# Selective-scan steps of 16 channels by 8 states in place of 8 channels by 16 states

## The chip, the cores and the metric

The kernel runs on one core of a Trainium2 chip. The metric is the device time of one execution in microseconds (us). The kernel before takes 7516.72 us (median of three runs, 7508.94 to 7519.74). All data is float32.

## The reference, cut to what matters

Four layers follow each other on an image of 2 x 64 channels x 96 x 96 pixels. Layer 0 is a non-local attention block, layer 3 a dynamic 3x3 filter; the change leaves both alone. Layer 1 holds one Mamba block over the 9216 pixels of each image. Layer 2 holds four: a forward and a backward one along the columns, then a forward and a backward one along the rows (sequences of 96). Each Mamba block computes, per channel of 128 and per state of 16:

```python
xc = silu(conv1d(xm) + convd_b)                    # 128 channels
dt, Bm, Cm = split(x_proj(xc), [4, 16, 16])
dt = softplus(dt @ dt_proj_w.T + dt_proj_b)        # 128 channels
A = -exp(A_log)                                    # 128 x 16
def step(h, inp):                                  # h: channels x states
    dA_t, dBx_t, C_t, x_t = inp
    h = exp(dt_t[:, None] * A) * h + dt_t[:, None] * B_t[None, :] * x_t[:, None]
    return h, einsum("ds,s->d", h, C_t)
y = (scan of step) + xc * Dp
out = (y * silu(z)) @ out_proj_w.T
```

## The kernel before

The sequence axis is the free axis. A *unit* is 768 positions (`CH`) of one Mamba block; there are 24 units in layer 1 and 96 in layer 2, 48 of them over columns and 48 over rows. In layer 2 units come in pairs, forward and backward, that share one image and one normalised input, so `image_0`, `image_1`, `norm_mean`, `norm_root`, `norm_scale` and the tail run once per pair; in layer 1 they (or `norm_centre`, `norm_square`, `norm_affine`) run for every unit. Below, an even unit is the first of a pair.

The recurrence of 128 channels x 16 states is 2048 rows, but an engine has 128 partitions. A unit is therefore worked off in 16 *steps* (`STEPS`), eight for each half of its positions (`HALF`, 384). A step of the kernel before has 8 channels by 16 states in each of its two 384-element parts. For each step:

- SyncE issues two DMAs (`read`, L912) that bring dt and dt times x of the step's channels from a DRAM copy (`rows`) to the tile `spread` (6 buffers);
- ScalarE makes the decay exp(dt A) with two exponentials (`decay`, L919) into the tile `h` (9 buffers), three steps ahead (`DECAY`);
- VectorE multiplies by B (`inputs`, L929): it reads `spread` and the PSUM bank `B`, and writes one of two PSUM tiles `place`, even steps one, odd steps the other; both products of a pair of steps stand before its two scans;
- VectorE runs the recurrence (`scan`, L944; L940 in layer 1), h = h * decay + place, in place in `h`;
- GpSimd multiplies h by C (L945);
- TensorE adds the states up into the PSUM bank `y` (`gather`, L954) with a 128x128 product for each part, two steps late, and first, once a half, the product with D (L951).

The bank `B` is filled by TensorE twice a unit (`shared`, L923), after the last product that reads its old content.

Everything else that a unit needs is cut into pieces with an offset in steps (`PIECES`, L995): a piece at offset o of a unit is issued at that unit's first step plus o, so that several units are in work at once. `run` (L1035) writes this order out by hand, step by step, and each engine takes its own instructions in this order. Pieces whose name is in `reads` come before the others of the same step. Offset -27, say, stands at step 5 of the unit two before. The pieces on the path of the softplus are `step_mm`, `step_read`, `step_exp` (three ScalarE operations), `step_log`, then on GpSimd `step_kept`, `step_sum`, `step_dt` (its sums) and `step_u` (dt times x), then `step_write` (L891, two DMAs to `rows`).

All matrix products outside `B`, `y` and `place` share one PSUM tile `m`: `open` hands it out, and the next product into it waits until ScalarE has read the last one. Eight PSUM banks are in use: four for `place`, one for `B`, one for `y`, two for `m`.

Of the kernel before, what the change touches and what calls it, by code (L numbers as in the profile page):

```python
# [35 lines left out]
NMAMBA = 5  # L36

# [34 lines left out]
def setup(ctx, tc, x, cols, mats, dtw):  # L72
# [42 lines left out]
    k.minus = const.tile([P, 1], FP, name="minus")  # L115
    nc.vector.memset(k.minus, -1.0)
# [91 lines left out]
def layer0_direct(k, scale, bias, pre):  # L208
# [9 lines left out]
    with (  # L218
# [19 lines left out]
        def product(lhsT, rhs, m, n):  # L238
            p = bank("m")[:m, :n]
            nc.tensor.matmul(p, lhsT=lhsT, rhs=rhs, start=True, stop=True)  # L240
            return p
# [321 lines left out]

class Carver:
# [16 lines left out]
def mamba_tables(k, pool):  # L581
# [4 lines left out]
    G = P // 8  # L586
    t = SimpleNamespace()

    t.member = pool.tile([P, 8], FP, name="member")
    nc.vector.reduce_sum(t.member, k.ident.rearrange("p (g i) -> p i g", i=8), axis=AX.X)  # L590
    t.group = pool.tile([P, 2, G], FP, name="group")
    for j in range(2):
        nc.vector.reduce_sum(t.group[:, j], k.ident.rearrange("p (g i) -> p g i", i=8), axis=AX.X)

    pair = pool.tile([P, 2, P], FP, name="pair")
    nc.vector.tensor_copy(pair, k.ident.unsqueeze(1).to_broadcast([P, 2, P]))
    pair = pair.rearrange("p j c -> p (j c)")
    t.gather = [pair[:, P - 8 * n : 2 * P - 8 * n] for n in range(G)]

# [8 lines left out]
def scratch(k, t, pool):  # L608


    G = P // 8
    t.turned = pool.tile([P, G, G], FP, name="turned")
    two = t.group.rearrange("p j g -> p (j g)")
    for n in range(G):
        k.nc.vector.tensor_copy(t.turned[:, n], two[:, G - n : 2 * G - n])
    t.placed = pool.tile([P, D_STATE, 8], FP, name="placed")
    t.rates = pool.tile([P, P // 8, P // 8], FP, name="turned_rates")


def mamba_weights(k, w, pool, product, tables, i):  # L620
# [4 lines left out]
    G = P // 8  # L625


# [3 lines left out]
    nc.vector.tensor_mul(  # L631
        tables.placed,
        tables.member.unsqueeze(1).to_broadcast([P, D_STATE, 8]),
        a.unsqueeze(2).to_broadcast([P, D_STATE, 8]),
    )
    p = product(tables.placed.rearrange("p s i -> p (s i)"), tables.group[:, 0], P, G)
    yield
    nc.vector.tensor_mul(tables.rates, tables.turned, p.unsqueeze(1).to_broadcast([P, G, G]))
    w.rates = pool.tile([P, G], FP, name=f"rates{i}")
    nc.vector.reduce_sum(w.rates, tables.rates, axis=AX.X)  # L640
# [23 lines left out]
    bc = pool.tile([P, 2, D_STATE, 8], FP, name=f"bc{i}")  # L664
    for j in range(2):
        at = DT_RANK + j * D_STATE
        nc.vector.tensor_copy(bc[:, j], x_w[:, at : at + D_STATE].unsqueeze(2).to_broadcast([P, D_STATE, 8]))
    w.gate_w = in_w[:, P:]
    w.bc = [bc[:, j].rearrange("p s i -> p (s i)") for j in range(2)]
# [5 lines left out]
class Mamba:  # L675
# [15 lines left out]
    STEPS = P // 8  # L691
    READ = 5
    DECAY = 3

# [14 lines left out]
    def product(self, lhsT, rhs, m, n):  # L709
        p = self.ps_m.tile([P, 2 * NB], FP, tag="m", name="mm")[:m, :n]  # L710
        self.nc.tensor.matmul(p, lhsT=lhsT, rhs=rhs, start=True, stop=True)
        return p
# [137 lines left out]
    def step_read(self, u):  # L850
# [5 lines left out]
        u.kept = self.by_half(self.work("kept", bufs=1))  # L856
# [4 lines left out]
    def step_exp(self, u):  # L861
        nc = self.nc
        nc.scalar.activation(u.e, u.e, AF.Exp, scale=-1.0)
        nc.scalar.activation(u.kept, u.e, AF.Identity, bias=1.0)
        nc.scalar.activation(u.kept, u.kept, AF.Identity, bias=self.k.minus)  # L865
# [5 lines left out]
    def step_kept(self, u):  # L871
        self.nc.gpsimd.tensor_sub(u.kept, u.e, u.kept)  # L872

    def step_sum(self, u):
        self.nc.gpsimd.tensor_add(u.log, u.log, u.kept)
# [159 lines left out]
    def run(self, units, first, n_first, other):  # L1035


        for u in units:
            u.dtu, u.h = {}, {}
# [340 lines left out]
```

## Time and profile before

| | us |
|---|---|
| median of three runs | 7516.72 |
| profiled execution, time | 7506.74 |
| profiled execution, span | 7504.8 |
| attention (layer 0), about the first 2440 of the span | 2440 |
| Mamba units (layers 1 and 2), up to about 7420 | 4980 |
| VectorE busy in the stretch 3500 to 7300 (3800 us) | 3786.7 |
| GpSimd busy in the same stretch | 3582.1 |
| TensorE busy in the same stretch | 3333.8 |
| ScalarE busy in the same stretch | 3042.1 |

The span runs from the first to the last instruction; the time has a few us around it. Busy times of one engine don't overlap with themselves, but those of different engines do. A mean duration of one instruction is longer than the distance at which the engine takes the next one, because the engines start an instruction before the last has drained: where work stands back to back, the distance from start to start is what counts, and a timeline shows it.

### The profile page before, as it was taken

How to read it: one execution, taken by the hardware profiler on the slowest of the kernel's cores; microseconds unless marked ns; L12 is line 12 of the kernel's file. 1: busy time of each engine (PE TensorE's matmuls, PEld its weight loads, DVE VectorE, ACT ScalarE, POOL GpSimd, SP SyncE). 2: the span in 40 equal slices, each digit the busy share in tenths (PEclk: the TensorE clock that was granted, in tenths of full speed). 3: DMA queues.
4: the chain of work that ended last, by engine and by line, in shares of the span. 5: the costliest groups of instructions: out<-in, count | busy, mean ns of one | idle time of the engine just before them, and what ended most of it. 6: DMA issues, size and time to landing. Idle time of an engine off the chain costs nothing.

```text
span 7504.8 us, 104657 instructions
## 1 busy us (share of the span) xinstructions
PE 6801.0 (91%) x34802; PEld 3032.7 (40%) x34802; DVE 6906.7 (92%) x5972; ACT 5303.9 (71%) x7420; POOL 4855.2 (65%) x3218
## 2 busy tenths in 40 slices
PE   9999999999998888888888888888988888888887
PEld 3333333333333344444444444444444444444443
DVE  6777877888886899999999999999999999999999
ACT  5555555555555778777877788888888787787783
POOL 0000000000001799998999999999999999999995
PEclk9999999999998999999999999999999999999999
DMA  1000000000000889998999999999999999999995
GB/s 46 1 1 1 1 1 1 3 5 6 5 6 30 292 320 336 320 326 302 352 331 344 343 354 355 347 355 350 352 355 352 349 353 350 353 353 346 351 356 198
DMA packets 593910, 1727.49 MB, mean 230 GB/s; under 512 B 65992, under 2 KB 67148, under 8 KB 592848
## 3 DMA queue, kind: packets, MB, share of 16 engines
q1 hardware_dynamic: 591912, 1717.69, 62.9%
q8 instruction: 275, 4.51, 0.2%
q10 hardware_dynamic: 1448, 3.04, 0.1%
q14 instruction: 275, 2.25, 0.1%
HBM read 1522.68 MB, written 197.79 MB: 229 GB/s over the span
## 4 chain that ended last, share of the span: by engine, by line
PE 10%; DMA 10%; issue 10%; POOL 9%; ACT 7%; DVE 6%; SPq 1%; DVEq 0%; ACTq 0%; POOLq 0%
DMA spread<-rows 8%; POOL h L945 6%; PE y L954 6%; ACT h L919 3%; DMA rows<-dtu 2%; DVE place L929 2%; DVE h L944 2%; PE mm L725 2%; PE conv L827 1%; POOL dtu L878 1%; PE y L951 1%; DVE xa L1279 1%; POOL dtu L882 1%; SPq L912 0%; PE B L923 0%
## 5 line engine op out<-in xcount | busy, mean ns | idle before, releaser
L945 POOL TENSOR_TENSOR h<-h,C 128x768 f32<-128x768 f32 x1920 | 3455.5, 1821 | 231.3 <-DVE h L944 197.0
L954 PE MATMUL y<-h,pair 128*128 128x384 f32 x7680 | 2818.1, 508 | 170.0 <-POOL h L945 168.5
L944 DVE TENSOR_TENSOR_SCAN h<-h,place 128x768 f32<-128x768 f32 x1536 | 2608.2, 1742 | 0.0
L919 ACT ACTIVATE h<-spread,xa 128x384 f32<-128x384 f32 x3072 | 1755.0, 608 | 481.0 <-DMA spread<-rows 441.3
L954 PEld LDWEIGHTS y<-h,pair 128*128 128x128 f32 x7680 | 1480.1, 198 | 1400.7 <-POOL h L945 418.2
L312 ACT ACTIVATE e<-f_exp 128x1024 f32<-128x1024 f32 x1296 | 1257.7, 1022 | 987.6 <-PE f_exp L298 987.6
L929 DVE TENSOR_TENSOR place<-spread,B 128x768 f32<-128x768 f32 x1920 | 1736.5, 953 | 96.2 <-PE B L923 48.6
L323 PE MATMUL y<-e,xb 64*64 64x512 f32 x10368 | 1232.1, 590 | 0.0
L298 PE MATMUL f_exp<-theta,phi 64*64 64x512 f32 x10368 | 1230.0, 589 | 2.0 <-DVE xb L283 1.5
L401 DVE TENSOR_TENSOR acc_e<-acc_e,e 128x1024 f32<-128x1024 f32 x612 | 771.6, 1261 | 300.7 <-ACT e L312 283.3
L337 POOL TENSOR_TENSOR ys<-ys,y_one 128x512 f32<-128x512 f32 x36 | 46.0, 1277 | 1456.2 <-DVE ys L336 1456.2
L410 DVE TENSOR_TENSOR acc_e<-acc_e,e 128x1024 f32<-128x1024 f32 x612 | 810.7, 1325 | 65.2 <-DVE acc_e L401 1.8
L940 DVE TENSOR_TENSOR_SCAN h<-h,state,place 128x384 f32<-128x384 f32 x768 | 714.6, 993 | 3.2 <-ACT h L919 3.1
L323 PEld LDWEIGHTS y<-e,xb 64*64 64x64 f32 x10368 | 393.6, 133 | 728.2 <-issue 722.4
L298 PEld LDWEIGHTS f_exp<-theta,phi 64*64 64x64 f32 x10368 | 395.5, 133 | 715.0 <-issue 703.0
L362 POOL TENSOR_TENSOR xa<-xa,t_att 64x512 f32<-64x512 f32 x36 | 54.3, 1508 | 755.9 <-ACT t_att L360 735.2
L919 ACT ACTIVATE h<-spread,rates 128x384 f32<-128x384 f32 x768 | 433.9, 608 | 113.1 <-DMA spread<-rows 99.8
L951 PE MATMUL y<-raw,xa 128*128 128x384 f32 x384 | 207.2, 626 | 213.3 <-ACT yg L961 185.7
L827 PE MATMUL conv<-xn,xa 64*128 64x384 f32 (+3 forms) x1536 | 275.3, 497 | 11.8 <-DVE xa L1161 4.1
L725 PE MATMUL mm<-raw,xa 128*128 128x384 f32 x768 | 279.4, 486 | 0.1
L872 POOL TENSOR_TENSOR kept<-dtu,kept 128x768 f32<-128x768 f32 x120 | 218.6, 1822 | 64.9 <-ACT kept L865 64.2
L832 ACT ACTIVATE raw<-conv,cols 128x768 f32<-128x768 f32 x120 | 108.2, 901 | 187.2 <-PE conv L827 143.5
(219 smaller groups left out, 5622.5 us busy)
## 6 DMA issues: line engine op xcount, KB each, us to landing
spread<-rows SPq DMA_DIRECT2D x3840, 384.0 KB, 5.6
rows<-dtu SPq DMA_DIRECT2D x240, 768.0 KB, 5.1
image<-pre SPq DMA_DIRECT2D x11, 384.0 KB, 2.3
xb<-image SPq DMA_DIRECT2D x11, 384.0 KB, 7.1
xa<-in_x SPq DMA_DIRECT2D x1, 2304.0 KB, 22.5
out<-xa ACTq DMA_DIRECT2D x7, 240.0 KB, 2.0
out<-xa SPq DMA_DIRECT2D x1, 1200.0 KB, 4.3
xa<-in_x SPq DMA_DIRECT2D x3, 384.0 KB, 11.6
```

What stands on the lines that cost most here:

```text
L298: nc.tensor.matmul(f[rows_of(half), bass.ts(side, NB)], lhsT=phi[at, m * P + half * C : m * P + (half + 1) * C], rhs=theta[at, bass.ts(i, ...
L312: nc.scalar.activation(e, f, AF.Exp)
L323: nc.tensor.matmul(ys[half][rows_of(side)], lhsT=g[at, m, :], rhs=e[at, bass.ts(side, NB)], start=m < 2, stop=m >= KEYS - 2,)
L401: nc.vector.tensor_add(block.acc, block.acc, es[0])
L410: nc.vector.tensor_add(block.acc, block.acc, es[1])
L725: self.nc.tensor.matmul(o, lhsT=lhsT, rhs=x, start=n == 0, stop=n == len(terms) - 1)
L919: self.nc.scalar.activation(h[:, bass.ts(q, HALF)], dt, AF.Exp, scale=u.w.rates[:, n : n + 1])
L929: self.nc.vector.tensor_mul(bx, x, self.B.unsqueeze(1).to_broadcast([P, 2, HALF]))
L940: nc.vector.tensor_tensor_scan(h[:, at], h[:, at], bx[:, at], state[:, q : q + 1], ALU.mult, ALU.add)
L944: nc.vector.tensor_tensor_scan(h[:, way], h[:, way], bx[:, way], 0.0, ALU.mult, ALU.add)
L945: nc.gpsimd.tensor_mul(h2, h2, u.C[:, bass.ts(half, HALF)].unsqueeze(1).to_broadcast([P, 2, HALF]))
L954: self.nc.tensor.matmul(self.y, lhsT=self.t.gather[n], rhs=rhs, start=False, stop=stop)
```

## The change

A step now has 16 channels (`SPAN`) by 8 states (`GROUP`) in each part. The two halves of the states are `PARTS`: steps 0 to 3 of a half take the first eight states of all channels, steps 4 to 7 the last eight.

- The tile `spread` of a half's step m serves step m and step m + 4, so a unit has 16 DMA reads instead of 32; each reads 16 rows and repeats each eight times. `rows` is written once.
- `B` and C have two patterns. TensorE fills `B` four times a unit, and C is made in two pieces (`c_mm_0`, `c_mm_1`), one for each half of the positions, with a ScalarE copy each.
- The states of a part are added up by products with 32 output rows, written to four 32-row quarters of `y`; the gathers of two steps are issued together, at odd steps.
- The softplus sums (e - kept etc.) are no longer three GpSimd operations: TensorE multiplies four terms with the identity (`sum_mm`, eight products) and ScalarE copies the sum back (`sum_read`). The kept term is made with its sign turned.
- For steps 7 and 15 (`ASIDE`) the product with B is made by GpSimd, three steps ahead. [...] The product goes to the SBUF tile `bx`, and the decay of these steps goes to `place`, one step ahead.
- The offsets of most pieces change.

Not shown: the tables and weights of the new layout (`mamba_tables`, `scratch`, `by_state`, `mamba_weights`), which are made once, and the state tile of layer 1, whose shape follows.

```diff
+SPAN, BLOCKS, PARTS = 16, 8, 2
+GROUP = P // SPAN
+TILE = 32
...
+def products(nc, p, lhsT, rhs, m, n):
+    each = lhsT if isinstance(lhsT, list) else [lhsT]
+    for j, one in enumerate(each):
+        nc.tensor.matmul(p[:m, j * n : (j + 1) * n], lhsT=one, rhs=rhs, start=True, stop=True)
+    return p[:m, : len(each) * n]
+def channels(block):
+    first = TILE * (block % 4) + SPAN * (block // 4)
+    return slice(first, first + SPAN)
...
+    held = pool.tile([P, 3 * SPAN], FP, name="held")
+    nc.vector.memset(held, 0.0)
+    own = k.ident.rearrange("p (i g) -> p i g", g=GROUP)
+    nc.vector.reduce_sum(held[:, SPAN : 2 * SPAN], own, axis=AX.X)
+    t.gather = [held[:, SPAN:], held[:, :TILE]]
...
-    STEPS = P // 8
-    READ = 5
+    STEPS = 16
+    READS = {2: 0, 3: 1, 5: 2, 6: 3}
     DECAY = 3
+    ASIDE = (7, 15)
...
+    def sum_mm(self, u):
+        u.p = self.mm([(self.k.ident, lambda j, t=t: t[:, j]) for t in (u.e, u.kept, u.log, u.dt)])
+    def sum_read(self, u):
+        self.nc.scalar.copy(u.dt, self.by_half(u.p))
...
-        u.rows = self.dram.tile([2 * P, 2 * CH], FP, tag="rows", name="rows")
-        for j in range(2):
-            self.nc.sync.dma_start(out=u.rows[j * P : (j + 1) * P], in_=u.both)
-    def c_mm(self, u):
-        u.p = self.mm([(u.w.bc[1], self.halves(u.xc))])
-    def c_read(self, u):
-        u.C = self.work("C")
-        self.nc.scalar.copy(u.C, u.p)
+        u.rows = self.dram.tile([P, 2 * CH], FP, tag="rows", name="rows")
+        self.nc.sync.dma_start(out=u.rows, in_=u.both)
...
+    def c_mm(self, u, half):
+        sides, u.p = self.open()
+        for part, p in enumerate(sides):
+            x = u.xc[:, bass.ts(half, HALF)]
+            self.nc.tensor.matmul(p, lhsT=u.w.bc[1][part], rhs=x, start=True, stop=True)
+    def c_read(self, u, half):
+        u.C[half] = self.by_half(self.work("C"))
+        self.nc.scalar.copy(u.C[half], self.by_half(u.p))
...
-    def read(self, u, step):
-        half, turns = self.turns(step)
-        u.dtu[step] = self.work("spread", 2 * CH, bufs=6)
-        for q, n in enumerate(turns):
-            row = u.rows[8 * n : 8 * n + P, bass.ts(half, CH)]
-            self.nc.sync.dma_start(out=u.dtu[step][:, bass.ts(q, CH)], in_=row)
+        part, m = divmod(m, BLOCKS // 2)
+        return half, part, m
+    def read(self, u, half, m):
+        d = u.dtu[half, m] = self.work("spread", 2 * CH, bufs=6)
+        for q in range(2):
+            rows = u.rows[channels(2 * m + q), bass.ts(half, CH)]
+            self.nc.sync.dma_start(
+                out=d[:, bass.ts(q, CH)], in_=rows.unsqueeze(1).to_broadcast([SPAN, GROUP, CH])
+            )
+    def spread(self, u, step, a):
+        half, _, m = self.turns(step)
+        return u.dtu[half, m].rearrange("p (q a t) -> p q a t", q=2, a=2)[:, :, a]
+    def place(self, step):
+        return self.places[step % 2][1].rearrange("p (q t) -> p q t", q=2)
+    def room(self, u, step):
+        u.h[step] = self.by_half(self.work("h", bufs=9))
+        u.decay[step], u.bx[step] = u.h[step], self.place(step)
+        if step in self.ASIDE:
+            u.decay[step], u.bx[step] = self.place(step), self.by_half(self.work("bx", bufs=1))
     def decay(self, u, step):
-        h = u.h[step] = self.work("h", bufs=9)
-        for q, n in enumerate(self.turns(step)[1]):
-            dt = u.dtu[step][:, q * CH : q * CH + HALF]
-            self.nc.scalar.activation(h[:, bass.ts(q, HALF)], dt, AF.Exp, scale=u.w.rates[:, n : n + 1])
-    def shared(self, u, half):
-        self.nc.tensor.matmul(self.B, lhsT=u.w.bc[0], rhs=u.xc[:, bass.ts(half, HALF)], start=True, stop=True)
-    def inputs(self, u, step):
-        bx = self.places[step % 2][1].rearrange("p (q t) -> p q t", q=2)
-        x = u.dtu[step].rearrange("p (q a t) -> p q a t", q=2, a=2)[:, :, 1]
-        self.nc.vector.tensor_mul(bx, x, self.B.unsqueeze(1).to_broadcast([P, 2, HALF]))
+        _, part, m = self.turns(step)
+        dt = self.spread(u, step, 0)
+        for q in range(2):
+            rate = u.w.rates[:, part, 2 * m + q : 2 * m + q + 1]
+            self.nc.scalar.activation(u.decay[step][:, q], dt[:, q], AF.Exp, scale=rate)
+    def shared(self, u, half, part):
+        x = u.xc[:, bass.ts(half, HALF)]
+        self.nc.tensor.matmul(self.B, lhsT=u.w.bc[0][part], rhs=x, start=True, stop=True)
+    def b_copy(self, u):
+        u.B = self.work("Bs", HALF, bufs=1)
+        self.nc.scalar.copy(u.B, self.B)
+    def inputs(self, u, step, engine, B):
+        B = B.unsqueeze(1).to_broadcast([P, 2, HALF])
+        engine.tensor_mul(u.bx[step], self.spread(u, step, 1), B)
...
     def gather(self, u, step):
-        half, turns = self.turns(step)
-        if turns[0] == 0:
+        half, part, m = self.turns(step)
+        if part == m == 0:
             self.nc.tensor.matmul(self.y, lhsT=u.w.direct, rhs=u.xc[:, bass.ts(half, HALF)], start=True, stop=False)
-        for q, n in enumerate(turns):
-            rhs, stop = u.h[step][:, bass.ts(q, HALF)], n == self.STEPS - 1
-            self.nc.tensor.matmul(self.y, lhsT=self.t.gather[n], rhs=rhs, start=False, stop=stop)
...
+            block = 2 * m + q
+            y = self.y[bass.ts(block % 4, TILE)]
+            stop = part == PARTS - 1 and block >= BLOCKS // 2
+            self.nc.tensor.matmul(y, lhsT=self.t.gather[block // 4], rhs=u.h[step][:, q], start=False, stop=stop)
...
-        (-56, "image_0"),
+        (-54, "image_0"),
+        (-53, "norm_centre"),
         (-52, "image_1"),
-        (-51, "norm_centre"),
-        (-49, "norm_square"),
+        (-52, "norm_square"),
         (-47, "norm_mean"),
-        (-45, "norm_root"),
+        (-46, "norm_root"),
         (-38, "norm_scale"),
         (-36, "norm_affine"),
         (-27, "conv"),
         (-25, "conv_read"),
-        (-25, "gate_mm"),
-        (-23, "gate_read"),
-        (-22, "silu"),
-        (-21, "step_mm"),
+        (-23, "gate_mm"),
+        (-21, "gate_read"),
+        (-21, "silu"),
+        (-20, "step_mm"),
         (-19, "step_read"),
         (-18, "step_exp"),
-        (-17, "step_kept"),
         (-17, "step_log"),
-        (-17, "c_mm"),
-        (-15, "c_read"),
-        (-15, "step_sum"),
-        (-11, "step_dt"),
-        (-9, "step_u"),
-        (-6, "step_write"),
+        (-16, "sum_mm"),
+        (-15, "sum_read"),
+        (-14, "step_u"),
+        (-11, "step_write"),
+        (-1, "c_mm_0"),
+        (0, "c_read_0"),
+        (2, "c_mm_1"),
+        (3, "c_read_1"),
+        (3, "b_copy"),
         (10, "y_half"),
+        (11, "b_copy"),
         (18, "y_read"),
         (19, "y_gate"),
-        (25, "tail_0"),
-        (26, "tail_1"),
-        (27, "tail_read"),
+        (23, "tail_0"),
+        (23, "tail_1"),
+        (25, "tail_read"),
...
         for n in range(begin, len(steps) + end + 1):
             s = n % self.STEPS
-            if at(n + self.READ):
-                self.read(*at(n + self.READ))
+            if s % 8 in self.READS and at(n - s % 8 + 8):
+                u, step = at(n - s % 8 + 8)
+                self.read(u, step // 8, self.READS[s % 8])
+            if at(n + 1) and at(n + 1)[1] in self.ASIDE:
+                self.decay(*at(n + 1))
             if at(n + self.DECAY):
-                self.decay(*at(n + self.DECAY))
+                u, step = at(n + self.DECAY)
+                self.room(u, step)
+                if step in self.ASIDE:
+                    self.inputs(u, step, self.nc.gpsimd, u.B)
+                else:
+                    self.decay(u, step)
+            pieces(n, False)
             if at(n):
                 u = at(n)[0]
                 if s % 2 == 0:
-                    self.inputs(u, s)
-                    self.inputs(u, s + 1)
+                    for step in (s, s + 1):
+                        if step not in self.ASIDE:
+                            self.inputs(u, step, self.nc.vector, self.B)
                 self.scan(u, s)
-                if s == 6:
-                    self.shared(u, 1)
+                if s % 4 == 2 and s < 14:
+                    self.shared(u, *divmod(s // 4 + 1, PARTS))
             if s == 14 and at(n + 2):
-                self.shared(at(n + 2)[0], 0)
-            for late in self.lates(s):
-                if at(n - late):
-                    self.gather(*at(n - late))
-            for late in (False, True):
-                for is_late, offset, name in table[s]:
-                    i = (n - offset) // self.STEPS
-                    if is_late == late and (0 if n >= 0 else 1) <= i < len(units) and units[i]:
-                        getattr(self, name)(units[i])
-                if s in self.OTHER and n >= 0 and not late:
-                    next(other, None)
+                self.shared(at(n + 2)[0], 0, 0)
+            if s % 2 and at(n - 2):
+                self.gather(*at(n - 3))
+                self.gather(*at(n - 2))
+            if s in self.OTHER and n >= 0:
+                next(other, None)
+            pieces(n, True)
```

More of the change, by code (lines that the diff above doesn't have):

```diff
@@ L238, in product @@
         def product(lhsT, rhs, m, n):
-            p = bank("m")[:m, :n]
-            nc.tensor.matmul(p, lhsT=lhsT, rhs=rhs, start=True, stop=True)
-            return p
+            return products(nc, bank("m"), lhsT, rhs, m, n)
         def projections(theta, phi, g, sides):
```

127 lines of the change are left out of this document (63 added, 64 removed).

## The prediction

> **What bounds the kernel now.** First the busy times by stretch (length, then busy us and instructions of PE, PEld, DVE, ACT, POOL, then PEclk, DMA share, GB/s), for a stretch in layer 2:
>
> ```profile
> 4500.00:5500.00 1000.00, 884.77 (x2660) 440.16 (x2659) 997.83 (x796) 815.57 (x1215) 950.44 (x561) 0.96 0.96 352
> ```
>
> VectorE never rests (998 of 1000), GpSimd, DMA and TensorE come close, ScalarE has 18% to spare. Then VectorE's timeline (start, length, then what):
>
> ```profile
> 5003.68 1.81 DVE L929 TENSOR_TENSOR place<-spread,B 128x768 f32<-128x768 f32 x2
> 5005.38 3.39 DVE L944 TENSOR_TENSOR_SCAN h<-h,place 128x768 f32<-128x768 f32 x2
> 5008.69 1.81 DVE L929 TENSOR_TENSOR place<-spread,B 128x768 f32<-128x768 f32 x2
> ```
>
> From start to start: two products 1.70, two scans 3.31, so 0.85 and 1.655 each and 40.1 for a unit's 16 steps. In layer 1 two steps take 5.35 (four half scans 3.64), 42.8 a unit. Of ScalarE and TensorE I need the same distances, for their queues:
>
> ```profile
> 5003.12 0.84 ACT L863 ACTIVATE dtu<-dtu 128x768 f32<-128x768 f32 x1
> 5003.99 0.84 ACT L864 ACTIVATE kept<-dtu 128x768 f32<-128x768 f32 x1
> 5004.87 0.94 ACT L865 ACTIVATE kept<-kept,minus 128x768 f32<-128x768 f32 x1
> 5005.71 1.10 ACT L919 ACTIVATE h<-spread,xa 128x384 f32<-128x384 f32 x2
> 5006.73 0.83 ACT L869 ACTIVATE log<-dtu 128x768 f32<-128x768 f32 x1
> 5007.46 2.12 ACT L919 ACTIVATE h<-spread,xa 128x384 f32<-128x384 f32 x4
> 5009.48 0.78 ACT L898 COPY C<-mm 128x768 f32<-128x768 f32 x1
> 5010.16 1.12 ACT L919 ACTIVATE h<-spread,xa 128x384 f32<-128x384 f32 x2
> ...
> 5029.78 1.28 ACT L841 ACT_TABLE_LOAD   x1
> 5031.07 1.49 ACT L841 ACTIVATE raw<-raw 128x1536 f32<-128x1536 f32 x1
> 5032.58 1.28 ACT L842 ACT_TABLE_LOAD   x1
> 5033.87 1.12 ACT L919 ACTIVATE h<-spread,xa 128x384 f32<-128x384 f32 x2
> 5035.02 1.61 ACT L990 ACTIVATE xb<-mm,cols 64x768 f32<-64x768 f32 x1
> ```
>
> The exponentials of a step ("decay") take 1.02, e and kept 2.59 (5003.12 to 5005.71), the logarithm 0.73, a copy from PSUM 0.68, silu with its two table loads 4.09.
>
> ```profile
> 5003.85 1.45 PE L725 MATMUL mm<-raw,xa 128*128 128x384 f32 x4
> 5005.14 2.74 PE L954 MATMUL y<-h,pair 128*128 128x384 f32 x8
> ...
> 5029.18 1.50 PE L725 MATMUL mm<-yg,xa 128*64 128x384 f32 x4
> 5030.61 1.48 PE L725 MATMUL mm<-xb,xa 64*64 64x384 f32 x2
> ```
>
> A product is two instructions: two products 1.29, so 0.645 each; a half of the tail over columns 2 x 1.41. A handover between engines is 0.2: conv's 16 instructions, 5019.38 on, end at 5022.11 by their distance, and ScalarE starts at 5022.31.
>
> **What the change takes from VectorE.** Two products a unit: 2 x 0.85 = 1.70, and nothing is added, so 38.4 in layer 2. Over 120 units that is 204 us, if VectorE never waits. The rest of this part is whether it does.
>
> **GpSimd.** Three sums go, two products come: at 1.77 from start to start, 16 times C, two products, dt times x, the gate and half a norm are 20.5 x 1.77 = 36.3 of 38.4. It has room.
>
> **DMA.** Half the reads and writes; the share 0.96 falls to about a half. VectorE waited for `spread` only 47 us in all (the group's line), so at most that is won, at least nothing: ScalarE's DMA waits (441 us) lay beside a busy VectorE. I take 0. Against it stands that the reads for m = 2 and 3 wait for the products of steps 4 and 5 and that `step_write` stands between them in SP's queue; the slack of about three steps (7 us) before ScalarE needs them covers the 5.6 to landing, and the excess over it would be paid once a half without it.
>
> **The gathers.** Four products on four quarters of the array's columns. No row has 128x32. Two ends: all serial, 4 x 0.645 = 2.6; all at once, 0.65. Nearest row, 64x64 products on four quarters in layer 0:
>
> ```profile
> 1000.38 1.90 PE L298 MATMUL f_exp<-theta,phi 64*64 64x512 f32 x16
> 1002.10 1.90 PE L323 MATMUL y<-e,xb 64*64 64x512 f32 x16
> ```
>
> 16 instructions in 1.72, 0.107 each for 512 columns, where a full-size one of 480 columns takes 0.419 (L1270, 126 in 52.8). Eight are 0.86; 384 columns would make it 0.64, and I keep 0.85, with something for the change of shape. TensorE falls from 35.5 a unit (0.885 x 40.1) by 32 x 0.645 - 8 x 0.85 = 13.8 and gains twelve products, 7.7: 29. It is no bound as a whole. ScalarE gains a second copy of C (0.68), `sum_read` (0.8) and two `b_copy` (0.36 each): 0.816 x 40.1 + 2.2 = 34.9 of 38.4. It fits as a whole too, but no longer with much room. The new tables cost some tens of small operations once, beside attention and in the fill of the first unit; within 10 either way, taken as 0.
>
> **The new loop through step 4.** `B` now changes every four steps, and the built program of the changed kernel makes VectorE's product of step 4 (and of 12) wait for ScalarE's `b_copy`, which reads the same bank. This copy stands in strict order behind everything ScalarE issues before it. ScalarE can't run ahead as it did, either: the decay of step 15 goes to `place`, free only when scan 13 has ended. From that moment:
> - ScalarE: decay of 15, then of 1, e and kept, decay 2, logarithm, decay 3, copy of C: 4 x 1.02 + 2.59 + 0.73 + 0.68 = 8.1
> - TensorE: `sum_mm` (waits for that copy, both use `m`) 8 x 0.645 = 5.2, gathers 0.85, `B` 0.75, C 1.29: 8.1
> - ScalarE: end of a decay begun meanwhile 0.3, copy of C 0.68, `b_copy` 0.36: 1.3
> - four handovers 0.8.
>
> Together 18.3. VectorE has in that time the product of 14, two scans, and steps 0 to 3: 0.85 + 3.31 + 10.02 = 14.2. Stall 4.1 in even units. In odd units `norm_mean` stands before `B`, waits for `sum_read` (0.3 more than the gathers) and takes 0.85; its logarithm must be read before C's product (0.5 more), and its exponential and the copy of y stand before C's copy (0.5): 2.2, so 6.3. Layer 1 has the norm in every unit: 20.5 against 0.85 + 3.64 + 10.7 = 15.2, stall 5.3.
>
> **The loop through step 12.** From the end of scan 5, which frees `place` for step 7's decay, ScalarE has in order: decays 7, 9, 10; conv's read 0.8; decays 11, 12; the tail's read 1.6; decay 13; y 0.4; image 1.55; decay 14; gate 0.68; silu 4.09; `b_copy` 0.36. Seven decays are 7.1, all 16.6. VectorE has the product of 6, two scans, steps 8 to 11: 14.2. The tail's read also waits: decay 12 is done some 6 after scan 5; the tail starts after C of step 5, which GpSimd reaches some 4 late (dt times x, gate and the step 7 product stand before it in steps 2 to 4), and takes 4 x 1.41 = 5.7: about 10, so 4.2 of waiting, with handovers 4.5. Stall 2.4 + 4.5 = 6.9 in even units over columns. Over rows the copies are short (0.85 and 0.8 for 1.6 and 1.55) and the tail 4.2: 4.0. In odd units there is neither tail nor image: 13.5 and about 0.9 of waiting for y, 0.2 over. Layer 1: 1.0.
>
> **The sum.** Over columns a pair: 4.1 + 6.3 + 6.9 + 0.2 - 3.4 = 14.1, 24 pairs: +338. Over rows: 4.1 + 6.3 + 4.0 + 0.2 - 3.4 = 11.2: +269. Layer 1: 5.3 + 1.0 - 1.7 = 4.6, 24 units: +110. In all +717 on the profiled execution's 7506.7: 8224; the median lies 10 above that execution, so 8234.
>
> Unknown prices: exponentials into PSUM and scans with PSUM first (nearest rows L919, 0.61, and L944, 1.74; a tenth either way on 34 exponentials and four scans is below 2 a unit). All of ScalarE 5% quicker: 0.45 in the first loop and 0.8 in the second, about -95; 5% slower the same up. Handovers of 0.1 or 0.3: about -/+ 0.5 a loop, 80 in all. Together some 250 either way.
>
> [...]
>
> **Rivals.**
> - *No stall* (0.07): ScalarE keeps enough lead. Its 18% of slack and the end of DMA waits speak for it, the two sums against. It needs the first loop below 14.2. 7516.7 - 204 = 7313.
> - *The copy is not what ends* (0.12): if the first loop ended at `B` itself, 18.3 falls by C's product, the copies and two handovers to about 15.4: 1.3 even, 3.6 odd, 2.7 in layer 1. Step 15's decay is then late in even units instead, 5.9 over columns and 3.6 over rows, and `B` for step 12 1.5 over columns. Pairs 8.9 and 5.1, layer 1 +1.0: +360, 7877.
> - *Gathers one after another* (0.08): 1.75 more per group; one lies in the first loop (120 x 1.75 = 210), one before each tail and each y (about 160): 8600.
> - *As forecast* (0.71): 8234, its own range 7980 to 8480. *Within 0.2%* (0.02), a chance meeting of gain and stall.
>
> **How the numbers follow.** The range takes the unknown prices and reaches to the second rival's 7877 above: 7850 to 8560, with under 2 in 10 outside. Faster 0.07, same 0.02, slower 0.91; 0.2% (15 us) is about what this kernel's runs can tell.
>
> **What would show it.** VectorE's busy share falls to about 0.83, with idle time before L977 at steps 4 and 12, put to ScalarE's copy L973; a unit over columns lasts 45 and 50 in turn. `sum_mm` takes 5.2 on end. The groups of four take 0.85. ScalarE waits for the tail. Wrong if VectorE stays above 0.95, or if its waits end at `B` L969 or at a decay L964.

## The result: 12% slower, in the two waits forecast

| kernel | median | lowest to highest |
|---|---|---|
| before | 7515.8 us (4 runs) | 7508.9 to 7519.7 |
| after | 8439.6 us (4 runs) | 8417.9 to 8449.7 |

The ratio is 1.1226, with a 95% interval of 1.1203 to 1.125. The profiled execution of the changed kernel took 8436.1 (span 8434.3), 929 more than that of before; the forecast's sum was 717.

The first view is the same stretch of layer 2 as before (length, busy us and instructions of PE, PEld, DVE, ACT, POOL, granted clock, DMA share, GB/s):

```profile
4500.00:5500.00 1000.00, 722.44 (x2723) 266.43 (x2722) 793.74 (x617) 704.61 (x1086) 749.08 (x441) 0.83 0.56 146
```

VectorE had 998 and has 794. Nothing has taken its place: every engine is less busy, the DMA share has fallen from 0.96 to 0.56, and TensorE's granted clock from 0.96 to 0.83. With no engine and no DMA queue full, the engines must be waiting for one another. The groups name the waits (busy, mean ns of one, then idle time ahead of them and what ended it):

```profile
L977 DVE TENSOR_TENSOR place<-spread,B 128x768 f32<-128x768 f32 x1680 | 1529.0, 949 | 1131.0 <-ACT Bs L973 993.2
...
L969 PE MATMUL B<-raw,xa 128*128 128x384 f32 x960 | 524.9, 634 | 743.7 <-DVE place L977 739.3
...
L742 PE MATMUL mm<-dtu,ident 128*128 128x384 f32 x960 | 436.6, 561 | 291.4 <-ACT C L915 288.9
...
L964 ACT ACTIVATE place<-spread,xa 128x384 f32<-128x384 f32 x384 | 224.6, 585 | 548.8 <-DVE h L991 542.4
L893 ACT COPY dtu<-mm 128x768 f32<-128x768 f32 x120 | 95.8, 799 | 670.3 <-PE mm L742 670.3
```

Read from the first line on: VectorE waits 993 us for ScalarE's copy of B to SBUF (`b_copy`, L973), which GpSimd's products of steps 7 and 15 read; ScalarE waits 670 for the sum on TensorE and 542 for a scan of VectorE; TensorE waits for both. VectorE's timeline, over columns, shows where in the unit (idle time ahead in brackets):

```profile
4722.54 1.83 DVE L977 TENSOR_TENSOR place<-spread,B 128x768 f32<-128x768 f32 x2 [1.53 <-ACT Bs L973]
...
4727.58 0.94 DVE L977 TENSOR_TENSOR place<-spread,B 128x768 f32<-128x768 f32 x1
4728.65 1.75 DVE L991 TENSOR_TENSOR_SCAN h<-h,place 128x768 f32<-128x768 f32 x1
4730.32 1.73 DVE L991 TENSOR_TENSOR_SCAN h<-place,bx 128x768 f32<-128x768 f32 x1
4731.97 1.80 DVE L977 TENSOR_TENSOR place<-spread,B 128x768 f32<-128x768 f32 x2
4733.68 3.39 DVE L991 TENSOR_TENSOR_SCAN h<-h,place 128x768 f32<-128x768 f32 x2
4736.99 1.80 DVE L977 TENSOR_TENSOR place<-spread,B 128x768 f32<-128x768 f32 x2
...
4747.36 1.83 DVE L977 TENSOR_TENSOR place<-spread,B 128x768 f32<-128x768 f32 x2 [5.27 <-ACT Bs L973]
...
4773.25 1.83 DVE L977 TENSOR_TENSOR place<-spread,B 128x768 f32<-128x768 f32 x2 [6.34 <-ACT Bs L973]
...
4799.87 1.83 DVE L977 TENSOR_TENSOR place<-spread,B 128x768 f32<-128x768 f32 x2 [7.06 <-ACT Bs L973]
```

The four waits are step 12 of an odd unit, step 4 and step 12 of an even one and step 4 of an odd one: 0.2, 4.1, 6.9 and 6.3 in the forecast. The lines between show something that the forecast had not: a pair of steps with both products on VectorE takes 5.02 (4731.97 to 4736.99), and a pair with one of them on GpSimd 4.39 (4727.58 to 4731.97). A product taken away is worth 0.63, not 0.85, since a single product isn't followed as closely (1.07) as two in a row (1.71).

TensorE's timeline ahead of the wait at 4747.36 shows the sum, its eight products and what follows:

```profile
4735.92 1.65 PE L742 MATMUL mm<-dtu,ident 128*128 128x384 f32 x2 [2.47 <-ACT C L915]
4737.36 1.49 PE L742 MATMUL mm<-kept,ident 128*128 128x384 f32 x2
4738.64 1.16 PE L742 MATMUL mm<-log,ident 128*128 128x384 f32 x2
4739.64 1.45 PE L742 MATMUL mm<-dtu,ident 128*128 128x384 f32 x4
4740.93 0.81 PE L742 MATMUL mm<-kept,ident 128*128 128x384 f32 x2
4741.57 0.81 PE L742 MATMUL mm<-log,ident 128*128 128x384 f32 x2
4742.22 0.81 PE L742 MATMUL mm<-dtu,ident 128*128 128x384 f32 x2
4742.95 0.85 PE L1004 MATMUL y<-h,held 128*32 128x384 f32 x8
4743.74 0.91 PE L969 MATMUL B<-raw,xa 128*128 128x384 f32 x2
```

From start to start, the last products take 0.64 each and the first two 1.44 and 1.28: half the speed, behind 2.47 us of standing still. The sum takes 7.03 and not 5.2. Over the 118 sums that TensorE's next product follows at once it takes 6.44 in the mean, and it goes with the granted clock, which the trace records: 5.37 at full clock throughout (48 sums), 6.98 where 2.9 to 3.4 us of the sum lay at half the clock (57), 8.03 where more did (13). The four narrow gathers do run beside one another: 0.79 for a group (4742.95 to 4743.74).

### The profile page after: what moved, and what is told of

Read it like the earlier page. It is cut to its first block, busy times and chain, and to the rows that moved or that the text cites. A ratio compares the mean times of both kernels' runs of the same rounds, so it can differ in the third digit from the quotient of the medians.

```text
span 8434.3 us, 103901 instructions
## 1 busy us (share of the span) xinstructions
PE 6689.8 (79%) x37692; PEld 2461.1 (29%) x37692; DVE 6741.0 (80%) x5710; ACT 5479.8 (65%) x7900; POOL 4664.4 (55%) x3098
## 4 chain that ended last, share of the span: by engine, by line
ACT 24%; PE 16%; DVE 13%; issue 7%; DMA 4%; POOL 3%; SPq 1%; DVEq 0%; ACTq 0%; POOLq 0%
PE mm L742 12%; ACT h L964 9%; DVE place L977 6%; DVE h L991 5%; DMA spread<-rows 4%; POOL h L993 2%; ACT C L915 2%; ACT L859 1%; DVE h L986 1%; ACT L858 1%; PE conv L844 1%; ACT dtu L893 1%; ACT Bs L973 1%; PE conv L838 1%; ACT log L887 1%
## 5 line engine op out<-in xcount | busy, mean ns | idle before, releaser
L977 DVE TENSOR_TENSOR place<-spread,B 128x768 f32<-128x768 f32 x1680 | 1529.0, 949 | 1131.0 <-ACT Bs L973 993.2
L991 DVE TENSOR_TENSOR_SCAN h<-h,place 128x768 f32<-128x768 f32 x1344 | 2289.3, 1739 | 25.1 <-DVE place L977 0.5
L964 ACT ACTIVATE h<-spread,xa 128x384 f32<-128x384 f32 x2688 | 1483.1, 606 | 142.9 <-DMA spread<-rows 141.9
L1004 PE MATMUL y<-h,held 128*32 128x384 f32 x7680 | 1147.1, 590 | 144.4 <-POOL h L993 144.3
L969 PE MATMUL B<-raw,xa 128*128 128x384 f32 x960 | 524.9, 634 | 743.7 <-DVE place L977 739.3
L338 POOL TENSOR_TENSOR ys<-ys,y_one 128x512 f32<-128x512 f32 x36 | 45.9, 1274 | 1458.4 <-DVE ys L337 1458.4
L742 PE MATMUL mm<-dtu,ident 128*128 128x384 f32 x960 | 436.6, 561 | 291.4 <-ACT C L915 288.9
L964 ACT ACTIVATE place<-spread,xa 128x384 f32<-128x384 f32 x384 | 224.6, 585 | 548.8 <-DVE h L991 542.4
L977 POOL TENSOR_TENSOR bx<-spread,Bs 128x768 f32<-128x768 f32 x240 | 435.9, 1816 | 168.8 <-issue 159.4
L969 PEld LDWEIGHTS B<-raw,xa 128*128 128x128 f32 x960 | 168.2, 220 | 1096.5 <-ACT place L964 686.3
L1004 PEld LDWEIGHTS y<-h,held 128*32 128x32 f32 x7680 | 207.5, 116 | 923.1 <-POOL h L993 516.0
```

Of the source, the lines that this page charges most:

```text
L742: self.nc.tensor.matmul(o, lhsT=lhsT, rhs=x, start=n == 0, stop=n == len(terms) - 1)
L964: self.nc.scalar.activation(u.decay[step][:, q], dt[:, q], AF.Exp, scale=rate)
L977: engine.tensor_mul(u.bx[step], self.spread(u, step, 1), B)
L991: nc.vector.tensor_tensor_scan(*flat, 0.0, ALU.mult, ALU.add)
L1004: self.nc.tensor.matmul(y, lhsT=self.t.gather[block // 4], rhs=u.h[step][:, q], start=False, stop=stop)
```

## The experiments

Each is an edit of the changed kernel, run once unless a number of runs is given; the changed kernel's own four runs lie within 32 us. In the expectations, 7.0 for the sum is the value of the two sums first read, in place of the mean 6.44.

**Is it the copy?** The copy moves behind VectorE's products, GpSimd's products with it:

```diff
-        (3, "b_copy"),
+        (4, "b_copy"),
-        (11, "b_copy"),
+        (12, "b_copy"),
@@ run: GpSimd's products two steps ahead instead of three
+            if at(n + 2) and at(n + 2)[1] in self.ASIDE:
...
+                self.inputs(u, step, self.nc.gpsimd, u.B)
...
```

> Edit: ScalarE's copy of B is issued one step later, behind VectorE's products of steps 4 and 12 instead of ahead of them, and GpSimd's products of steps 7 and 15 one step later with it; the work is the same. Theory (VectorE loses its time in the two waits for this copy, and the first is longer than forecast because the sum on TensorE takes 7.0 us and not 5.2): the forecast's rival without this wait gave 7877 with a sum of 5.2; 1.8 us more in each of 120 units is 216, so about 8090 (7950 to 8250), and the idle time of VectorE put to the copy, 993 us, falls below 100. Rival (the copy only stands in front of a B that is as late): 8380 to 8470, the idle time the same in sum and put to B's product on TensorE.

Measured 8042.3, inside the theory's range; VectorE's group in this run:

```profile
L977 DVE TENSOR_TENSOR place<-spread,B 128x768 f32<-128x768 f32 x1680 | 1526.9, 947 | 649.2 <-PE B L969 449.1 <-ACT Bs L973 146.3 <-DMA spread<-rows 53.7
```

The waits for the copy fall from 993 to 146, not below 100: in step 14 of even units the product now waits for the copy (4.0 in the mean over columns, 1.7 over rows). And B itself turns up as the next late thing, 449. The copy did end the wait, by some 400 us; behind it stood B, as in the forecast's second rival (7877).

**Is it the products on GpSimd?** Without them there is no copy at all:

```diff
-    ASIDE = (7, 15)
+    ASIDE = ()
-        (3, "b_copy"),
-        (11, "b_copy"),
```

> Edit: the products of steps 7 and 15 go back to VectorE and the two copies of B go; VectorE has 1.70 more in every unit (204 in all). Theory (the waits for the copy cost more than the two products bring): nothing of VectorE's idle time is put to the copy any more; step 12 loses its stalls (of the 993 us on the copy about 290), step 4 about half of its own (B itself still stands behind the sum on TensorE; about 350), 204 come back: about 8000 (7850 to 8150). Rival (the copy only stands in front of a B that is as late): the stalls stay and the 204 are added, 8440 to 8640.

Measured 7974.4: VectorE has two products more in each unit and the kernel is 465 us faster. Of this run's group of products, the only long wait left is 482 for B:

```profile
L977 DVE TENSOR_TENSOR place<-spread,B 128x768 f32<-128x768 f32 x1920 | 1731.1, 947 | 536.3 <-PE B L969 482.2 <-DMA spread<-rows 54.0
```

**Is it the sum?** Two runs take it out of the way of step 4. In the first, B, C's second half and the copy go ahead of it:

```diff
-        (-16, "sum_mm"), (-15, "sum_read"), (-14, "step_u"), (-11, "step_write"),
+        (-14, "sum_mm"), (-13, "sum_read"), (-12, "step_u"), (-10, "step_write"),
-        (2, "c_mm_1"), (3, "c_read_1"), (3, "b_copy"),
+        (0, "c_mm_1"), (1, "c_read_1"), (2, "b_copy"),
```

> Edit: the sum on TensorE and its read move behind the B of step 4; C's second half, its copy and the copy of B stand ahead of it, dt times x and the write of the rows come two and one step later; the work is the same. Theory (the sum is what makes step 4 wait): the stalls of 5.3 to 7.1 us at step 4 fall to under 1, some 5.5 x 120 = 660 less, and with about a third given back at step 12 and in ScalarE's queue about 8000 (7850 to 8150). Rival (TensorE is late at step 4 whatever stands ahead of B, since its products wait for GpSimd's): 8350 to 8450.

In the second, GpSimd adds as before (`sum_kept`, `sum_log`, `sum_dt`, one `tensor_add` each) and the eight products go; dt times x then stands five steps later and the write of the rows four.

> Edit: dt is summed by three additions on GpSimd as in the kernel before, two steps later the write of the rows; the eight products of the sum on TensorE and ScalarE's copy of their result go. Theory (the sum on TensorE is most of the first stall): step 4's stalls fall to under 1.5; GpSimd has 36.3 + 3 x 1.77 = 41.6 us a unit and becomes nearly the bound; about 8030 (7900 to 8200). Rival (it is not the sum): 8350 to 8500.

Measured 7986.5 and 8023.7, both in the theory's range. In the first, over columns, step 4 waits 0 in even units and 0.4 in odd ones; in its place step 12 waits 8.6 and 1.9 in the mean, as the tail is late (ScalarE waits up to 7.6 for it ahead of the copy). In the second, step 4 still waits 1.8 (columns) and 2.0 (rows) in even units, where under 1.5 was expected. Of the 660 that the expectation took away, 453 stay away.

**Why is the sum slow?** Four products whose result is overwritten keep TensorE busy ahead of B in step 14:

```diff
+    def warm(self, u, count):
+        u.open = self.open()
+        for n in range(count):
+            self.nc.tensor.matmul(u.open[0][n % 2], lhsT=self.k.ident, rhs=u.xc[:, :HALF], start=True, stop=True)
...
```

> Edit: in step 14, ahead of B, four more products of 128x384 that write C's bank before C does (their result is overwritten); nothing else changes. Theory (the sum takes 7.0 us instead of 5.2 because TensorE runs at half its clock after it has stood still for 2 to 3 us): the sum falls to 5.2 to 6.2 and the time by 100 to 216 us, 8225 to 8340, though TensorE has more to do. Rival (the first products of the sum are slow for another reason, such as their operands): the sum stays at 7.0 and the time at 8420 to 8550.

Measured 8381.8: more work and 58 us faster, 36 below the lowest of the changed kernel's runs. The mean of the sum falls from 6.44 to 5.82, as the theory had it, which is 74 over 120 units. The time misses the theory's range (8225 to 8340): the four products now stand ahead of B, and VectorE's waits for B itself grow from 54 to 133. Where the idle time ahead is 0.89, in this run's TensorE timeline, it is the full-speed one, 5.36:

```profile
4752.80 0.91 PE L742 MATMUL mm<-dtu,ident 128*128 128x384 f32 x2 [0.89 <-ACT C L922]
4753.55 0.81 PE L742 MATMUL mm<-kept,ident 128*128 128x384 f32 x2
...
4758.16 0.85 PE L1011 MATMUL y<-h,held 128*32 128x384 f32 x8
```

The same operands at both speeds: the rival falls. The record of the granted clock says so directly. For the changed kernel's sum at 4735.92 and the five stretches around its start (columns as in the first view, the granted clock third from the end):

```profile
4725.70:4729.10 3.40, 0.43 (x2) 0.30 (x2) 3.27 (x4) 1.37 (x3) 3.40 (x3) 1.00 1.07 255
4729.10:4732.50 3.40, 3.40 (x12) 1.13 (x11) 3.40 (x3) 3.34 (x6) 2.77 (x3) 0.50 1.04 237
4732.50:4735.90 3.40, 0.95 (x3) 0.19 (x1) 3.40 (x4) 3.40 (x7) 1.58 (x1) 1.00 1.03 234
4735.90:4739.30 3.40, 3.38 (x6) 1.86 (x7) 3.40 (x4) 0.99 (x2) 3.35 (x2) 0.50 0.65 151
4739.30:4742.90 3.60, 3.60 (x12) 1.92 (x10) 2.79 (x2) 0.00 (x0) 2.02 (x2) 0.99 0.00 0
```

In the two stretches ahead of a halved clock TensorE (first busy time) worked for 0.43 and 0.95 of 3.40; in those ahead of a full one for 3.40 and 3.38. The halved clock agrees with the distances, 0.64 and 1.28. In the whole record the granted clock is 1 or 0.5 and nothing else, and none of the 342 stretches of each is shorter than 3.41. The idle times were shorter than that: 3.23 ahead of B at 4728.67 and 2.47 ahead of the sum were followed by the half clock, and the gathers and C's product between them (1.52 for 0.79, and a record of 2.12 for 1.45) ran slowly. How short an idle time still brings the half clock was not tried.

**Are the narrow gathers worth it?** Each as a product of 128x128 into the whole bank of `y`:

```diff
-            y = self.y[bass.ts(block % 4, TILE)]
-            self.nc.tensor.matmul(y, lhsT=self.t.gather[block // 4], rhs=u.h[step][:, q], start=False, stop=stop)
+            self.nc.tensor.matmul(self.y, lhsT=self.t.gather[block], rhs=u.h[step][:, q], start=False, stop=stop)
...
```

> Edit: each gather is a product of 128x128 into all rows of y, in place of 128x32 into a quarter; the sums are the same. Theory (four 128x32 run beside one another, 0.79 a group as measured, and TensorE is on the way to step 4): a group takes 2.6, so 1.8 more in one group of the first loop and in those before the tail and y, the 370 us that the forecast's rival had, 8810; if a busier TensorE keeps its clock up, the sum falls from 7.0 to 5.2 and 216 come off: 8590 to 8840. Rival (TensorE has room to spare and the narrow products bring nothing): 8400 to 8480.

Measured 8626.0. The gathers' busy time goes from 1147 to 2771, the granted clock from 0.887 to 0.962 over the span, the sum from 6.44 to 5.81. The loss is 186 where the forecast's rival had 370. The faster sum gives back 76 of that (0.63 in 120 units); where the other 108 are was not looked for.

**Where do the loops begin?** The forecast let them start with the decay of step 15 or 7, which waits for the scan that leaves `place`. With that decay in SBUF and issued with the others:

```diff
-            u.decay[step], u.bx[step] = self.place(step), self.by_half(self.work("bx", bufs=1))
+            u.bx[step] = self.by_half(self.work("bx", bufs=1))
@@ run
-            if at(n + 1) and at(n + 1)[1] in self.ASIDE:
-                self.decay(*at(n + 1))
...
```

> Edit: the decays of steps 7 and 15 go to their buffer in SBUF like all others, issued three steps ahead, instead of to the accumulator that scan 5 or 13 must leave first; nothing else. Theory (as the forecast has it, both loops begin when that scan ends, since ScalarE can't run ahead of it): the 513 us in which ScalarE waits for the scan ahead of this decay go, and with them about 1.5 us of stall a unit: about 8270 (8150 to 8370). Rival (this wait of ScalarE is only room it has anyway, and the stalls come from the sum and the tail alone): 8400 to 8460. Unknown: the scan with both operands in SBUF, 1.66 if it takes what the others do.

Measured 8600.1, outside both. Among SyncE's waits in the stretch 3600 to 7700 (total, times, longest) there now is GpSimd's product of steps 7 and 15, for which the changed kernel's reads never wait:

```profile
SPq L941 <- ACT h L964: 1537.1, 165, 15.9
SPq L941 <- DVE place L977: 915.4, 264, 9.7
SPq L941 <- POOL bx L977: 308.5, 161, 4.5
```

With the decay issued earlier, the buffer of another read was given back first, and the third read of each half now waited for GpSimd. The test had changed two things. With the first line of the edit alone:

> Edit: the decays of steps 7 and 15 go to their buffer in SBUF, but are issued where they were, one step ahead; the order of every queue and of the buffers of the reads stays as in the changed kernel, and only ScalarE's wait for scans 5 and 13 goes. (The run that also issued them three steps ahead let the third read of each half take the buffer that GpSimd's product of step 7 or 15 reads, so that SyncE waited for that product.) Theory (the wait for the scan is where both loops begin, and a part of the stalls): the 513 us of ScalarE's waits for the scan go, about 1.1 of a unit's stalls with them: about 8310 (8220 to 8390). Rival (this wait is only room that ScalarE has, and reads or the sum are late instead): 8400 to 8470.

Measured 8296.1, 144 less, as the theory had it. So the scan's wait is part of the loop, at 1.2 a unit. The scan with both operands in SBUF costs some of it back, by its group line 1953 ns in the mean where it took 1730 (139 of the 192 take 1732, the other 53 take 2533 in the mean; why was not tried):

```profile
L991 DVE TENSOR_TENSOR_SCAN h<-h,bx 128x768 f32<-128x768 f32 x192 | 375.0, 1953 | 0.0
```

**The second loop.** On top of the late sum, the copy for step 12 goes ahead of silu:

```diff
-        (10, "y_half"), (11, "b_copy"),
+        (10, "b_copy"), (11, "y_half"),
```

> Edit: the sum behind B as in the run with the late sum, and the copy of B for step 12 one step earlier, ahead of silu and of the copy of y; nothing else against that run (7987). Theory (with the sum out of the way what is left is step 12's copy, 4.1 us of silu and 1.5 of the image ahead of it): its stalls of 9.1 and 3.7 fall to under 4, and some of it comes back where silu is now late: 7870 to 7960. Rival (the tail's read, which still stands ahead, decides alone): 7970 to 8010.

Measured 8055.3, outside both and slower than without the edit (7986.5). The copy's waits fall from 562 to 239, but VectorE's scans of steps 7 and 15 have two new ones (layer 2, layer 1; for most of the second the profile names no releaser):

```profile
L991 DVE TENSOR_TENSOR_SCAN h<-place,bx 128x768 f32<-128x768 f32 x192 | 334.7, 1743 | 219.8 <-ACT place L964 215.8 <-PE y L1004 4.0
L986 DVE TENSOR_TENSOR_SCAN h<-place,state,bx 128x384 f32<-128x384 f32 x96 | 91.9, 999 | 114.9 <-issue 98.2 <-POOL h L993 16.7
```

What stood ahead of the copy (silu 4.1, the image 1.5) now stands ahead of the decay of step 15, for which scan 15 waits. In ScalarE's strict order the copy that went ahead handed its wait to the next instruction that is needed.

**Is there an order without waits?** One product on GpSimd (step 7), one copy, and all pieces set anew:

```diff
-    ASIDE = (7, 15)
+    ASIDE = (7,)
+        (-27, "gate_mm"), (-26, "conv"), (-22, "silu"), (-14, "sum_mm"), (-8, "step_u"), (-7, "step_write"),
+        (-2, "c_mm_0"), (-1, "c_mm_1"), (2, "b_copy"), (11, "y_half"), (25, "tail_0"), (27, "tail_read"),
...
```

> Edit: only step 7 is done by GpSimd; one copy of B, in step 2; the steps of the pieces are set anew: C early (steps 14 to 0), sum in step 2 behind B, gate ahead of conv, silu two steps earlier, the tail two steps later and read in step 11. The work is that of the changed kernel but for one product back on VectorE and one copy less. Theory (both stalls are a matter of what stands ahead of the copy of B and of B in two queues): VectorE has 40.1 - 0.85 = 39.25 a unit in layer 2, 7516.7 - 120 x 0.85 = 7415 without a stall, and with under 0.5 a unit left 7415 to 7480. Rival (the loops close elsewhere, because ScalarE or TensorE have too little room at any order): 7560 to 7900, with VectorE's idle time above 1.5 a unit.

Measured 7810.2, the rival's range, but with a cause that can be mended: ScalarE waits 571 us for reads in layer 2, and those stand in SyncE's queue behind a write of the rows that waits 1196 for GpSimd, by SyncE's waits:

```profile
SPq L905 <- POOL dtu L901: 1195.9, 95, 16.6
```

The write moves ahead, and others with it:

```diff
-        (-22, "silu"), (-8, "step_u"), (-7, "step_write"), (25, "tail_0"), (27, "tail_read"),
+        (-24, "silu"), (-12, "step_u"), (-10, "step_write"), (24, "tail_0"), (26, "tail_read"),
...
```

> Edit: the run with one product on GpSimd (7810), with the rows written a step and a half of a read earlier: dt times x in step 4, the write in step 6, both behind the sum's read in step 3; the norm, gate and silu again a step or two earlier. That run waited 572 us for reads that came behind a late write of the rows, and that is what is taken away. Theory (each queue has room once nothing slow stands ahead of the copy of B, of B and of the write): VectorE 39.25 a unit and stalls below 0.5: 7415 to 7480, faster than the kernel before. Rival (TensorE's low clock and ScalarE's 90% load leave no order without stalls): 7520 to 7750.

Measured 7517.6 (10 runs; 7510.2 for the kernel before, run alongside), ratio 1.0011 with an interval of 1.0002 to 1.0021: the whole loss is gone, and nothing is won. Its stretch of layer 2, and VectorE's group:

```profile
4500.00:5500.00 1000.00, 783.30 (x3234) 304.40 (x3236) 968.21 (x761) 839.12 (x1278) 850.59 (x502) 0.91 0.69 175
```

```profile
L977 DVE TENSOR_TENSOR place<-spread,B 128x768 f32<-128x768 f32 x1800 | 1626.5, 945 | 142.0 <-PE B L969 140.0
```

VectorE is at 968. One product less in 120 units is worth 120 x 0.63 = 76 and not the 102 that the expectation took. It is given back, and a little more, in two places: 46 ahead of the products (142 of idle time for 96 before; 25 of it at the start, where the two longest waits are 62.5 and 35.1 for 46.4 and 26.3) and 42 ahead of the table operations of layer 1 (L650 to L682; before, none above 1.5). A last run went after the waits for B:

```diff
-        u.p = self.mm([... for t in (u.e, u.kept, u.log, u.dt)])
+        self.nc.gpsimd.tensor_add(u.kept, u.kept, u.e)
+        u.p = self.mm([... for t in (u.kept, u.log, u.dt)])
-        (-52, "image_0"), (-52, "image_1"),
+        (-54, "image_0"), (-53, "image_1"), (-16, "sum_kept"),
...
```

> Edit: against the run with one product on GpSimd that came to the time of before (7517.6), one of the three additions of dt goes to GpSimd (kept + e, 1.77), which leaves six products of the sum on TensorE for eight, and the two image copies stand one and two steps earlier in ScalarE's queue. What is left there in VectorE's timeline is 1.04 (B behind the tail) and 1.7 (B behind the norm's mean, which waits for the image) in every pair of units in layer 2. Theory (both go, since the chain sum, gate, conv, tail is 1.3 to 1.8 shorter and the image is 2.5 earlier): 48 x 2.7 = 130 at most, about 7430 (7400 to 7480), faster than the kernel before. Rival (GpSimd, at 85%, or ScalarE is late instead): 7500 to 7570.

Measured 7515.0 (11 runs; before 7505.4), ratio 1.0015, 1.0006 to 1.0024: the rival's range. VectorE is at 975 of 1000 and the time doesn't move; VectorE's waits for B are 148 us where they were 140. What holds B up now was not looked for. No version was found that beats the kernel before.

## Why the forecast was right, and what it mis-sized

The mechanism was the forecast's: with the copy gone (7974), the copy later (8042) or the sum out of its way (7987, 8024), about half of the loss goes each time. All of it goes (7518) in a kernel with one of GpSimd's two products, one of the two copies and the pieces set anew; no run has both loops open with both products in place. *No stall* falls with the result. *Gathers one after another* falls with 0.79 a group. *The copy is not what ends* is half true: the copy ends the waits, but B is next, a few us behind, so that taking the copy away alone is worth 400 and not 900.

The stalls themselves, per unit, from VectorE's idle time ahead of its products (means of all units: 24 of layer 1, and over columns and over rows 24 even and 24 odd ones each):

| stall | forecast | measured |
|---|---|---|
| step 4, columns, even / odd | 4.1 / 6.3 | 4.28 / 5.67 |
| step 4, rows, even / odd | 4.1 / 6.3 | 4.64 / 5.94 |
| step 12, columns, even / odd | 6.9 / 0.2 | 6.62 / 0.91 |
| step 12, rows, even / odd | 4.0 / 0.2 | 3.87 / 1.26 |
| step 8, columns, even / odd | 0 / 0 | 0.54 / 0.68 |
| layer 1, steps 4 / 8 / 12 | 5.3 / 0 / 1.0 | 6.46 / 1.00 / 1.75 |

From its first product of layer 1 to its last of layer 2, VectorE is busy 4919.2 of 4973.4 us before and 4756.0 of 5893.0 after. So its idle time grows by 1083, where the forecast's stalls are 922 in all, and its work falls by 163, where the forecast has 204; and the first product comes 10 later (2456.4, before 2446.7). That is 161, 41 and 10: the 212 that the sum of 717 was short of 929. Of the 161, columns have 29 (18.7 a pair against 17.5, 24 pairs), rows 27 (15.7 against 14.6) and layer 1 70 (9.2 against 6.3, 24 units); 26 lie ahead of a new table operation (L650) in layer 1, whose tables were taken as 0, and the rest is in small waits.

The means at step 4 hide two sizes. In layer 2, 20 of the 48 even units wait 3.6 to 3.7 and 27 wait 5.0 to 5.3; 23 of the odd ones wait 5.4 and 20 wait 6.8 to 7.1. In every one of the longer kind the sum ran 2.9 to 3.4 us at half the granted clock, in none of the shorter kind. No unit of layer 2 stands near the 4.1 or the 6.3 of the forecast: that the means of layer 2 come so close is in part luck, since a loop forecast 0.5 to 0.9 too long at full clock met, in about half of the units, a half clock that it did not have, worth 1.7.

- *What the change takes from VectorE.* Mis-sized: the distance of two products in a row was halved, but what is left of the pair is a lone product, whose scan starts 1.07 after it (the last 0.13 of it counts as idle time above). The trace of before had only pairs.
- *The loop through step 4.* Its cover was right (14.2; 4778.3 to 4792.7 is 14.4) and ScalarE's first part too (8.1 from 4778.42 to the end of C's copy). The sum was mis-sized: 5.2 forecast, 6.44 in the mean, because the durations came from a TensorE that was busy for 885 us of 1000 at a granted clock of 0.96, and the change makes it wait ahead of the sum (2.47 at 4735.92; 722 of 1000 and 0.83 in the same stretch). Handovers of 0.1 and less, for 0.2, gave some of it back in layer 2. In layer 1 the sum takes 7.46, and the stall is 1.2 longer than forecast.
- *The loop through step 12.* Right over columns. What the forecast lacked is the wait for B at step 8: in one unit of layer 1 (at 2922), conv ran at half speed ahead of it (5.2, forecast 2.7), after waiting 4.8 for a table operation in VectorE's own queue. Whether all the waits at step 8 come from this was not tried.
- *DMA and GpSimd* were rightly taken as no bound: ScalarE's waits for reads between 3600 and 7700 fall from 430 us to 115. But the slack of "about three steps" is real: in the runs that took 8600 and 7810 it was used up, as the reads' buffers or the write came later.
- *What would show it.* VectorE's share was 0.79, forecast 0.83; the units last 45.9 and 52.5 from step 4 to step 4 (first product, 4701.46, to 4747.36 to 4799.87), forecast 45 and 50; ScalarE waits for the tail; `sum_mm` was not 5.2. The unknown prices were near: exponentials into `place` 585 ns (606 into SBUF), scans that read their decay there 1730 (1739).
- *The price of the second reader.* No run here tried the product of VectorE and the copy, which read the same bank, without the wait between them. The price of this wait stands in the runs: a copy of 0.48 us, 240 times, to which the profile puts 993 us of VectorE's waiting, though some 400 were won when the copy came later (8042) and 465 when it went with its products (7974).

## What to carry to other kernels

Before work is taken off a saturated engine, follow each value that it shares with the engine taking over, round to where it started: a lead of several steps can become a circle whose length, not any engine's load, is the time. Prices taken from a busy engine need not hold once it waits: here the distance of TensorE's products doubled, from 0.64 to 1.28, in stretches of 3.41 us and more. Taking one late instruction out of a strict queue was worth only the distance to the next late one, so the queue has to be laid out as a whole.

## What was not expected of the hardware

- TensorE doing more took less time: four useless products a unit, 58 us faster; full-size gathers raised the granted clock from 0.887 to 0.962, though that kernel was 186 slower.
- The stalls at step 4 come in two sizes, 1.7 us apart, by whether a stretch of half clock (3.4 us) falls on the sum.
- Of two products in a row on VectorE, 1.71 together, taking one away saved 0.63.
- A scan with both operands in SBUF took 1953 ns in the mean in one run (8296) and 1796 in another (8600), up to 3.15 us, with one in PSUM 1730.
